# A four-layer network on one core: the convolution and the routing issued from written-out tables, experts' results laid out by partition, keys scaled on VectorE, and idle products ahead of the last keys

## The chip, the cores and the metric

The kernel runs on one core of one Trainium2 chip. The metric is device time in microseconds (us). In this text PE is the tensor engine, DVE is VectorE, ACT is ScalarE, POOL is GpSimd and SP is the engine that issues most of the DMA transfers. All data are float32.

## The reference

The input x has 8 sequences of 512 tokens with 128 features, 4096 tokens in all. Each of four layers works on a layer norm of x, and its result is added to x.

```python
x = x + conv(layernorm(x))        # sequence convolution with per-position weights
x = x + fp4_ffn(layernorm(x))     # gated FFN with FP4 rounding of inputs and weights
x = x + ttt(layernorm(x))         # attention by test-time training
x = x + experts(layernorm(x))     # 8 experts, 2 per token

# conv, per head of 8 features, K = 31 taps
avg    = cumsum(x) / (1, 2, 3, ...)
energy = stt + sigmoid(gate) * dyn            # dyn, gate = avg @ W_pe + b_pe
w      = softmax(energy over the 31 taps), zero where the tap lies before the start
out    = sum over taps of w[tap] * avg shifted by tap
v      = layernorm(out @ W_fc.T + residual) * gamma + beta

# ttt
q, k, v = x @ qkv_w + qkv_b ; q, k divided by their norm per head, scaled and shifted
for _ in range(2):                            # two steps of gradients and Newton-Schulz
    theta = theta - 0.1 * newton_schulz(grad of mean((silu(k@gate) * (k@val) @ proj - v)**2))
o = (silu(q @ gate) * (q @ val)) @ proj @ proj_w + proj_b

# experts
logits = x @ Wg + bg ; the two best of 8, gates by softmax over these two
pos    = place of (choice, token) in its expert, first all first choices, then all second
keep   = pos < capacity                       # 1229 rows for each expert
ye     = gelu(rows @ W1 + b1) @ W2 + b2       # for the rows of each expert
out[token] = sum over its two choices of gate * keep * ye[its row]
```

## The kernel before

The 4096 tokens lie in on-chip memory as `cx.x`, 128 partitions by NT = 32 tiles of 128 features; G = 4 tiles make a group of 512 tokens, and there are NG = 8 groups. Token number n * 128 + p stands in partition p of tile n. `Line` objects (`vec`, `ten`, `act`, `gp`) chain the instructions of one engine in the order in which the program issues them, so the order of those calls is the order on the engine. Where no Line is used, a scheduler orders the instructions by their dependences.

The profiled execution goes through these stages (us from the start of the span): convolution 0 to 234, FP4 FFN 234 to 376, keys 376 to 408, gradients and Newton-Schulz twice 407 to 926, output of the attention with the routing 930 to 1059, experts 1061 to 1222, last loads, adds and stores 1222 to 1240.

**Convolution** (`sequence_conv`). The features of one sequence are spread over partitions as (head, tap), four tap groups g = 0 to 3 (NGR = 4, of which NP = 3 weights are held in PSUM too). One pass of the loop L603-658 handles sequence b and, on the way, parts of others: `nxt` = b+1, `then` = b+2, `old` = b-1. For `cur`: `shared` lets POOL do a part of the products base * weights (L472), `product` does the others on VectorE (L483), `add_up` sums them over the taps on PE (cv, L492, eight matmuls a call), `part_sums` and `sums` make the softmax's denominators on PE with a copy dn on ACT (L439), `invert` takes the reciprocal rs on VectorE (L448), and `turn_inverse` turns it (rb) and copies it on ACT (rbs, L457). For `nxt` and `then`: `gates` and `taps` (matmuls and tanh), `energy` (en and the running maximum top, L395), `turn_top`, `greatest` (mx, L405) and `turn_greatest` (the maximum over taps, mb), `less` (subtract it) and `weigh` (exp on ACT). For `old`: `scale_down`, `project`, `norm1` (with statistics L263), and `finish` for b-2. `add_beta`, `scaled`, `means` belong to the neighbours b, b+4 and b+3. The sequence of these calls is written out in the loop by hand.

**Keys** (in `ttt`, L1236-1263). For each group: the k and v product; squares on ACT and their sums on VectorE (nrm); the copy of v to on-chip memory on VectorE (L1249); the scaling kt of the group before on ACT (L1196, `adjusted`); the root on ACT; the copy of a turned input; the division, which gives k (L1177, VectorE); four transposes of k on PE (tp, L1191). The first gradient's first product is `pa` (L1489).

**Output of the attention and routing** (L1290-1329, `Moe.route` L1650-1742). For each group the products pa and pb with the updated weights, silu on ACT (sw), the gated product ht on VectorE (L1317), the output product o on PE (L1322) and x = o + x (L1327). `moe.route(g - 1)` stands in front of the output product: transposes of x, statistics, a reciprocal root by `rsqrt` (L87-95), the logits (PSUM tile `both`, shared with the place sums), normalized rows xr on ACT, the choice of the two best (L1691-1697), counts (L1708-1712), place sums (L1716), slots (L1717-1727), and eight indirect DMA transfers from POOL's queue that write the rows to their slots in DRAM (L1732). A row carries the number of its token (`num`) and its gate. The transfers of second choices go first; each of those of first choices waits for the second choices of the group before (`after`).

**Experts** (`Moe.experts`, L1751-1865). For each expert its rows are loaded (`load`), in pieces of four tiles turned (`turn`: transposes and the copy xt, L1819), multiplied with W1 (ph, L1831), Gelu on ACT (ht), multiplied with W2 (po, L1844), biased and weighted on VectorE (ye, L1854 and L1856), and written by an indirect DMA of POOL's queue for each tile of 128 rows (L1858) to the row of its token: in `res` for the first six experts (one half for each choice), in an `own` buffer for each of the last two. The results are read back as y (L1805) and added to x (L1807): `behind` names the pieces after which this is done for res and the first own buffer, and a last loop does it for the last own buffer. Rows in res and own are in the order of the token numbers.

Of the kernel before, what the change touches and what calls it, by code (L numbers as in the profile page):

```python
# [1 line left out]

# [146 lines left out]
def sequence_conv(cx):  # L149
# [20 lines left out]
    BUSY = 14  # L170
    with ExitStack() as st:
# [430 lines left out]
        add_up(cur, 3)  # L602
        for b in range(1, B):  # L603
            cur, nxt, then, old = seq[b], seq.get(b + 1), seq.get(b + 2), seq.get(b - 1)
            shared(cur)
            product(cur, 0)
            if b > 1:
                finish(seq[b - 2], nc.gpsimd)
            part_sums(cur)
            sums(cur)  # L610
            if old:
                scale_down(old)
                project(old)
            add_up(cur, 0)
            if nxt:
                for g in (2, 3):
                    energy(nxt, g)
            invert(cur)
            if nxt:
                turn_top(nxt)  # L620
            if then:
                gates(then, 0)
            product(cur, 1)
            if nxt:
                greatest(nxt)
            turn_inverse(cur)
            if then:
                taps(then, 0)
            if nxt:
                turn_greatest(nxt)  # L630
            add_beta(b)
            add_up(cur, 1)
            if old:
                norm1(old, nc.gpsimd)
            if b + 4 < B:
                scaled(b + 4)
            if b == B - 3:
                ffn.load(flat(tri)[:, : ffn.NW], cur["spread"])
            if b >= B - 2:
                last_weights(cur)  # L640
                shared(cur, NP, NGR)
            product(cur, 2)
            add_up(cur, 2)
            if then:
                for g in (0, 1):
                    energy(then, g)
                gates(then, 1)
                taps(then, 1)
            if nxt:
                less(nxt)  # L650
                weigh(nxt, 0, 1)
            if b + 3 < B:
                seq[b + 3] = means(b + 3)
            if nxt:
                weigh(nxt, 1, NGR)
            if b < B - 1:
                product(cur, 3)
                add_up(cur, 3)
# [253 lines left out]
def fp4_ffn(cx):  # L912
# [7 lines left out]
        "H0 G2 H1 x0 G3 P0 T0 s0 S0 A2 A3 t0 H2 H3 D0 C0 P1 S1 d0 c0 T1 U0 D1 C1 T2 C2 g0 "  # L920
        "R0 R0 W0 K0 U1 f0 O0 u0 a0 f1 f2 W1 g1 K1 W2 K2 a1 W3 E0 K3 f3 K4 K5 K6 R1 K7 R1 "
        "r0 O1 r0 o0 "
# [210 lines left out]
def ttt(cx):  # L1133
# [10 lines left out]
    with ExitStack() as st:  # L1144
# [54 lines left out]
        with ExitStack() as s1:  # L1199
# [16 lines left out]
            FIRST, AHEAD = 4, 2  # L1216
# [23 lines left out]
            for g in range(NG):  # L1240
# [8 lines left out]
                vec(nc.vector.tensor_copy(grp(v, g), cur[:, :, D:]))  # L1249
                if g:  # L1250
                    act(adjusted(kt[:, (g - 1) * W : g * W], tk, 1))
# [4 lines left out]
                over_norm(cur[:, :, :D], root, nrm, grp(k, g), vec)  # L1256
                if g + AHEAD + 1 < NG:
                    normal(g + AHEAD + 1)
                tk = turn(ps, "t", grp(k, g), ten)
# [33 lines left out]
        with ExitStack() as s4:  # L1293
# [10 lines left out]
            for g in range(NG):  # L1304
                ht = p2.tile([P, NF, W], F32, tag="ht", name="ht")
                for c in range(NF):
                    pa = ps_h.tile([P, W], F32, tag="h", name="pa")
                    nc.tensor.matmul(
                        pa, gate[:, c * P : (c + 1) * P], qt[:, g * W : (g + 1) * W], start=True, stop=True
                    )  # L1310
                    pb = ps_h.tile([P, W], F32, tag="h", name="pb")
                    nc.tensor.matmul(
                        pb, val[:, c * P : (c + 1) * P], qt[:, g * W : (g + 1) * W], start=True, stop=True
                    )
                    sw = p2.tile([P, W], F32, tag="sw", name="sw")
                    nc.scalar.activation(sw, pa, AF.Silu)
                    nc.vector.tensor_tensor(ht[:, c, :], pb, sw, ALU.mult)  # L1317
                if g:
                    moe.route(g - 1)
                o = ps_o.tile([P, G, D], F32, tag="o", name="o")  # L1320
                for j in range(G):
                    for c in range(NF):  # L1322
                        nc.tensor.matmul(
                            o[:, j, :], ht[:, c, j * P : (j + 1) * P], w2[:, c, :],
                            start=(c == 0), stop=(c == NF - 1),
                        )
                nc.vector.tensor_tensor(grp(cx.x, g), o, grp(cx.x, g), ALU.add)  # L1327
            moe.route(NG - 1)
# [254 lines left out]

class Moe:
# [29 lines left out]
    def open_router(self, stack):  # L1614
# [27 lines left out]

        self.xr = cp.tile([P, K, NT, DX], F32, tag="xr", name="xr")
# [4 lines left out]
        self.seen = cp.tile([P, K, E], F32, tag="seen", name="seen")  # L1648
        nc.gpsimd.memset(self.seen, 0.0)
        self.limit = nc.gpsimd.to_reg(R - 1)  # L1650

    def route(self, g):
        cx = self.cx
        nc, tc, p2 = cx.nc, cx.tc, self.p2
# [266 lines left out]
```

## Time and profile before

| | |
|---|---|
| median of 3 runs | 1241.89 us (1241.77 to 1242.49) |
| profiled execution, its own time | 1242.03 us |
| its span on the core | 1240.3 us |
| mean granted PE clock | 0.965 |
| PE busy | 1097.9 us, 89% |
| VectorE busy | 754.0 us, 61% |
| POOL busy | 736.8 us, 59% |
| PE weight loads busy | 661.5 us, 53% |
| ACT busy | 488.0 us, 39% |

A share of busy time is a mean over all stages; the limit of a stage is seen only in a window of its own. A line of the timeline gives start and duration in us, the engine, the line of the kernel, the operation, output and inputs with their shapes, and in brackets the idle time before it and what ended it. A group of instructions gives the count, then the least, median and greatest duration in ns, and the first and last start. The clock is given as a share of full speed.

### The profile page before, as it was taken

The page shows a single profiled execution, that of the slowest core. Times are in us where ns is not written, and L with a number is a line of the kernel's source. Part 1 is how long each engine was busy: PE and PEld are TensorE (multiplying, and loading weights), DVE is VectorE, ACT ScalarE, POOL GpSimd, SP SyncE. Part 2 cuts the span into 40 slices and gives each one's busy share as a digit, 9 for nine tenths or more (in the row PEclk, how much of TensorE's full clock was granted, in tenths as well). Part 3 has the DMA queues.
Part 4 walks back from the last instruction along what each step waited for, and adds up shares of the span by engine and source line. Part 5 has one row for each costly group of instructions (what it writes and reads, how often), then busy time and mean ns, then how long its engine had stood idle before and what let it go on. Part 6 is the DMA issues. An engine that isn't in the chain of part 4 may idle for free.

```text
span 1240.3 us, 15590 instructions
## 1 busy us (share of the span) xinstructions
PE 1097.9 (89%) x5335; PEld 661.5 (53%) x5335; DVE 754.0 (61%) x1788; ACT 488.0 (39%) x1001; POOL 736.8 (59%) x720
## 2 busy tenths in 40 slices
PE   6999997858987899999988999999899993799992
PEld 4343432536666455555566455555576762577772
DVE  6899999988986544444455444444466785123354
ACT  4656554335657322232244232222343331243331
POOL 2266667635656888888822888888400656255553
PEclk9999999878999899999999999999999997799996
DMA  5324435860000000000000000000000111221277
GB/s 155 90 85 118 119 97 192 318 196 2 1 1 1 1 1 1 1 0 1 1 1 1 1 1 0 1 1 1 1 1 1 44 44 45 59 72 50 68 193 208
DMA packets 66894, 67.27 MB, mean 54 GB/s; under 512 B 6927, under 2 KB 48734, under 8 KB 66816
## 3 DMA queue, kind: packets, MB, share of 16 engines
q1 hardware_dynamic: 59296, 56.57, 15.3%
q0 software_dynamic: 4608, 8.43, 2.1%
q10 hardware_dynamic: 2912, 1.29, 0.4%
q8 instruction: 42, 0.69, 0.2%
q14 instruction: 36, 0.29, 0.1%
HBM read 40.00 MB, written 27.13 MB: 54 GB/s over the span
## 4 chain that ended last, share of the span: by engine, by line
PE 58%; DVE 21%; ACT 9%; issue 4%; POOL 3%; DMA 3%; ACTq 0%; DVEq 0%; POOLq 0%; SPq 0%
PE ph L1537 5%; PE sum L1512 5%; PE po L1844 4%; PE pp L1527 4%; PE sum L1511 4%; PE sum L1513 4%; PE ph L1831 4%; PE pa L1489 4%; PE pb L1491 4%; DVE v L858 3%; PE cv L492 2%; DVE pr L483 2%; PE pt L1520 2%; PE gu L974 1%; DVE ht L1317 1%
## 5 line engine op out<-in xcount | busy, mean ns | idle before, releaser
L1502 POOL TENSOR_TENSOR ds<-sw,s 128x512 f32<-128x512 f32 x64 | 81.7, 1276 | 86.3 <-DVE sw L1497 86.3
L1504 POOL TENSOR_TENSOR ds<-ds,s 128x512 f32<-128x512 f32 x64 | 111.6, 1744 | 5.0
L1732 POOL DMA_INDIRECT rows<-xr,slot x64 | 62.9, 983 | 73.8 <-DVE rs L95 45.1
L1495 ACT COPY b<-pb 128x512 f32<-128x512 f32 x64 | 37.5, 586 | 162.1 <-PE pb L1491 161.5
L1858 POOL DMA_INDIRECT res<-ye,xe x60 | 58.4, 974 | 66.2 <-DVE ye L1856 28.1
L472 POOL TENSOR_TENSOR pr<-base,en 128x512 f32<-128x512 f32 x52 | 74.9, 1474 | 36.9 <-ACT en L428 36.5
L1499 DVE TENSOR_TENSOR h<-sw,b 128x512 f32<-128x512 f32 x64 | 50.2, 785 | 70.6 <-ACT b L1495 70.1
L1834 ACT ACTIVATE ht<-ph,b 128x512 f32<-128x512 f32 (+2 forms) x100 | 56.1, 588 | 93.5 <-PE ph L1831 92.0
L483 DVE TENSOR_TENSOR pr<-base,w 128x3072 f32<-128x3072 f32 (+2 forms) x27 | 86.3, 3206 | 0.8 <-ACT w L426 0.8
L1503 POOL TENSOR_TENSOR ds<-sw,ds 128x512 f32<-128x512 f32 x64 | 82.8, 1294 | 5.0
L1505 POOL TENSOR_TENSOR ds<-ds,b 128x512 f32<-128x512 f32 x64 | 81.6, 1274 | 5.0
L1527 PEld LDWEIGHTS pp<-proj,ht 128*128 128x128 f32 x512 | 67.1, 191 | 30.7 <-issue 29.8
L1844 PE MATMUL po<-w,ht 128*128 128x128 f32 (+1 forms) x640 | 77.8, 278 | 0.0
L1522 ACT COPY ht<-pt 128x512 f32<-128x512 f32 x64 | 37.6, 587 | 101.5 <-PE pt L1520 101.5
L1497 DVE TENSOR_TENSOR sw<-pa,s 128x512 f32<-128x512 f32 x64 | 44.2, 691 | 53.7 <-ACT s L1493 53.7
L1831 PE MATMUL ph<-xt,w 128*128 128x512 f32 (+2 forms) x200 | 73.4, 511 | 3.4 <-DVE xt L1819 3.4
L1844 PEld LDWEIGHTS po<-w,ht 128*128 128x128 f32 (+1 forms) x640 | 74.6, 189 | 0.7
L1539 DVE TENSOR_TENSOR db<-ph,sw 128x512 f32<-128x512 f32 x64 | 44.2, 691 | 47.2 <-PE ph L1537 47.2
L1537 PE MATMUL ph<-proj_t,dpt 128*128 128x512 f32 x128 | 71.6, 641 | 0.0
L492 PE MATMUL cv<-pr,sel 128*32 128x512 f32 x512 | 62.4, 616 | 8.6 <-DVE pr L483 8.6
L1489 PE MATMUL pa<-gate,kt 128*128 128x512 f32 x128 | 66.8, 604 | 2.5 <-ACT b L1495 2.4
L1512 PE MATMUL sum<-db,k 128*128 128x512 f32 x128 | 66.2, 598 | 1.6 <-DVE db L1539 1.6
(359 smaller groups left out, 2545.6 us busy)
## 6 DMA issues: line engine op xcount, KB each, us to landing
base<-far SPq DMA_DIRECT2D x64, 268.0 KB, 5.2
rows<-empty SPq DMA_DIRECT2D x1, 5005.0 KB
res<-zero SPq DMA_DIRECT2D x1, 4096.0 KB, 26.3
own<-zero SPq DMA_DIRECT2D x2, 2048.0 KB, 18.8
w<-in_L_ffn_W SPq DMA_DIRECT2D x16, 256.0 KB, 4.8
y<-res SPq DMA_DIRECT2D x16, 256.0 KB, 5.5
xe<-rows SPq DMA_DIRECT2D x7, 585.0 KB, 4.3
y<-own SPq DMA_DIRECT2D x12, 256.0 KB, 4.7
```

Source lines behind the costliest of these rows:

```text
L483: vec(nc.vector.tensor_tensor(s["pr"][g][:, lo:hi, :], s["base"][:, lo:hi, at], w.to_broadcast([P, hi - lo, L]), ALU.mult))
L492: ten(nc.tensor.matmul(s["cv"][32 * j : 32 * (j + 1), :], sel[:, i].rearrange("p a h -> p (a h)"), s["pr"][g][:, i * NJ + j, :], start=(g ...
L1489: nc.tensor.matmul(pa, ki, gate, start=True, stop=True)
L1502: nc.gpsimd.tensor_tensor(ds, sw, s, ALU.mult)
L1503: nc.gpsimd.tensor_tensor(ds, sw, ds, ALU.subtract)
L1504: nc.gpsimd.tensor_tensor(ds, ds, s, ALU.add)
L1505: nc.gpsimd.tensor_tensor(ds, ds, b, ALU.mult)
L1512: nc.tensor.matmul(sums[1], ki, db, **kw)
L1527: nc.tensor.matmul(pp, ht[:, c * P : (c + 1) * P], proj[:, c, :], start=(c == 0), stop=(c == NF - 1))
L1537: nc.tensor.matmul(ph, dpt, proj_t, start=True, stop=True)
L1831: ten(nc.tensor.matmul(ph[:, :n], self.w1[:, e, c * P : (c + 1) * P], xt[:, :n], start=True, stop=True))
L1844: ten(nc.tensor.matmul(po[:m, i - lo, :], ht[:, c, (i - lo) * P : (i - lo) * P + m], self.w2[:, e, c, :], start=(c == 0), stop=(c == NF - ...
```

## The change

It has five parts.

1. The convolution's loop is issued from a table `ORDER`; a letter names the call, a digit its tap group. Against the old sequence, rs comes one energy earlier and mx behind the statistics of pj on VectorE; add_up of group 1 comes ahead of rb, ev and mb on PE; dn is copied ahead of four operations of `finish`, and the rows xn of `scaled` ahead of rbs, on ACT; the exps are taken in the order of groups 1, 3, 2.
2. Keys: kt of groups 0 to 6 is scaled by VectorE, the copy of v stands behind k, and twelve products of the identity with itself go ahead of the last group's transposes.
3. Output and routing are issued from two tables with Lines on three engines; `Moe.route` becomes a class `Route`. The last group is worked on in two halves. Three copies go from VectorE to ACT (the second set of rows, the second choice and the two gates), the logits have a PSUM tile of their own, and the wait of the first choices' transfers is taken by one memset on POOL ahead of them. A Gelu of one column is issued on ACT at the end of the stage.
4. Tokens are numbered p * 32 + n, so that the 4 tiles of a group in one partition are one stretch of 2 KB in res and own.
5. The last expert's first piece of four tiles becomes two pieces of two, and `behind` is adapted.

```diff
+    ORDER = (
+        "S0 P0 D0 n0 N0 F0 J0 e2 A0 v0 e3 t0 g0 g1 P1 A1 Z0 L0 X0 T0 P2 s0 i0 k0 k1 m0 B0 A2 E0 E1 g2 g3 "
+        "k2 k3 l0 w0 M0 w1 w3 w2 p3 a3 "
+    )
...
         for b in range(1, B):
             cur, nxt, then, old = seq[b], seq.get(b + 1), seq.get(b + 2), seq.get(b - 1)
-            shared(cur)
-            product(cur, 0)
-            if b > 1:
-                finish(seq[b - 2], nc.gpsimd)
-            part_sums(cur)
-            sums(cur)
...
+            parts = dict(
+                S=(cur, lambda s, g: shared(s)), p=(cur if b < B - 1 else None, product), P=(cur, product),
+                a=(cur if b < B - 1 else None, add_up), A=(cur, add_up), n=(cur, lambda s, i: part_sums(s)),
+                N=(cur, lambda s, i: sums(s)), v=(cur, lambda s, i: invert(s)), i=(cur, lambda s, i: turn_inverse(s)),
+                X=(cur if b >= B - 2 else None, lambda s, i: more_shared()),
+                D=(old, lambda s, i: scale_down(s)), J=(old, lambda s, i: project(s)),
+                Z=(old, lambda s, i: norm1(s, nc.gpsimd)), F=(seq.get(b - 2), lambda s, i: finish(s, nc.gpsimd)),
+                e=(nxt, energy), t=(nxt, lambda s, i: turn_top(s)), T=(nxt, lambda s, i: greatest(s)),
+                m=(nxt, lambda s, i: turn_greatest(s)), l=(nxt, lambda s, i: less(s)),
+                w=(nxt, lambda s, g: weigh(s, g, g + 1)),
+                g=(then, gate), k=(then, tap), E=(then, energy),
+                M=(b + 3 if b + 3 < B else None, lambda b, i: mean(b)), s=(b + 4 if b + 4 < B else None, lambda b, i: scaled(b)),
+                B=(b, lambda b, i: add_beta(b)), L=(b if b == B - 3 else None, lambda b, i: load_ffn()),
+            )
+            for name in ORDER.split():
+                at, part = parts[name[0]]
+                if at is not None:
+                    part(at, int(name[1]))
...
-            FIRST, AHEAD = 4, 2
+            FIRST, AHEAD, BUSY = 4, 2, 12
...
-                vec(nc.vector.tensor_copy(grp(v, g), cur[:, :, D:]))
                 if g:
-                    act(adjusted(kt[:, (g - 1) * W : g * W], tk, 1))
+                    vec(nc.vector.tensor_scalar(
+                        kt[:, (g - 1) * W : g * W], tk, cols[:, 1, 0:1], cols[:, 1, 1:2], ALU.mult, ALU.add
+                    ))
...
                 over_norm(cur[:, :, :D], root, nrm, grp(k, g), vec)
+                vec(nc.vector.tensor_copy(grp(v, g), cur[:, :, D:]))
                 if g + AHEAD + 1 < NG:
                     normal(g + AHEAD + 1)
+                if g == NG - 1:
+                    busy = ps.tile([P, W], F32, tag="t", name="busy")
+                    for _ in range(BUSY):
+                        ten(nc.tensor.matmul(busy[:, :P], cx.ident, cx.ident, start=True, stop=True))
                 tk = turn(ps, "t", grp(k, g), ten)
...
+            ORDER = (
+                "a2 t0 a4 H1 u0 a2 S1 l0 b1 G0 b8 H2 S2 b4 G1 b1 H3 n0 S3 n1 n2 n3 m0 c7 G2 c1 d4 G3 O0 "
+                "O1 d3 e6 v0 O2 O3 f6 x0 f2 h0 s0 "
+            )
+            LAST = (
+                "a1 H1 S1 t0 u0 a6 G0 H2 S2 a1 l0 b9 b4 G1 b1 H3 c1 S3 n0 n1 G2 c1 n2 n3 m0 G3 c2 O0 O1 "
+                "c4 d1 x0 T0 U0 d1 A1 d1 A1 d1 A2 d3 L0 e1 B1 e1 B1 e1 B1 e3 v0 B5 f1 B2 f1 B1 f1 B1 f1 "
+                "B1 f1 B1 N0 N1 C1 f1 C1 f2 C1 M0 C5 D7 E4 V0 F8 "
+            )
+            vec, ten, act = Line(tc), Line(tc), Line(tc)
+            parts = [(g * G, G) for g in range(NG - 1)] + [(NT - G, G // 2), (NT - G // 2, G // 2)]
...
+                parts = dict(zip(T, (lambda s, i, f=f: getattr(s["route"], f)() for f in ("turn", "turned", "logits", "spread", "sums"))))
+                parts[T[5]] = lambda s, j: s["route"].normal(j)
+                parts.update((c, step(name)) for c, name in zip(t, ("stats", "roots", "first", "second", "before", "places")))
...
+                table = dict(
+                    H=(s, hidden), S=(s, silu), G=(s, gated), O=(s, out_of), x=(s, lambda s, i: add(s)),
+                    h=(nxt, hidden), s=(nxt, silu), **routing(old, "abcdef", "tulmvn"),
+                    **(routing(s, "ABCDEF", "TULMVN") if nxt is None else {}),
+                )
...
+            ahead = wp.tile([P, 1], F32, tag="ahead", name="ahead")
+            act(nc.scalar.activation(ahead, cx.eps[1e-5], AF.Gelu_apprx_tanh))
...
+class Route:
...
+    def spread(self):
+        self.act(self.moe.cx.nc.scalar.copy(self.rows[1][:, :, :D], self.rows[0][:, :, :D]))
...
+        pl = m.ps_t.tile([P, W], F32, tag="t", name="pl")[:, : self.n * E]
...
+        self.act(nc.scalar.copy(self.hot[:, K], self.hot[:, K - 1]))
...
+            self.act(nc.scalar.activation(self.rows[k][:, :, D + 1], dif, AF.Copy, bias=0.5, scale=s))
...
+        for k in (1, 0):
+            if k == 0 and lo:
+                gate = nc.gpsimd.memset(self.small("gate", 1), 0.0)
+                m.after(gate, m.scatters[-1][: len(m.scatters[-1]) // K])
...
-        nc.gpsimd.iota(num, [[T, K], [P, NT]], base=0, channel_multiplier=1)
+        nc.gpsimd.iota(num, [[T, K], [1, NT]], base=0, channel_multiplier=NT)
...
-        res = self.slots.res.rearrange("(k n p) d -> p k n d", k=K, p=P)
-        sums = [res[:, k] for k in range(K)] + [t.rearrange("(n p) d -> p n d", p=P) for t in self.slots.own]
+        res = self.slots.res.rearrange("(k p n) d -> p k n d", k=K, p=P)
+        sums = [res[:, k] for k in range(K)] + [t.rearrange("(p n) d -> p n d", p=P) for t in self.slots.own]
...
-            for lo, hi in (((0, G), (G, 2 * G), (2 * G, NR)) if e < E - 1 else ((0, G), (G, G + 2), (G + 2, G + 4), (G + 4, NR)))
+            for lo, hi in (((0, G), (G, 2 * G), (2 * G, NR)) if e < E - 1 else ((0, 2), (2, G), (G, G + 2), (G + 2, G + 4), (G + 4, NR)))
...
-        behind = {first + i: (i // 2, i % 2) for i in range(2 * (K + OWN - 1))}
+        behind = {first + at: (i // 2, i % 2) for i, at in enumerate((0, 1, 2, 3, 5, 6))}
```

In the tables of part 3 the letters H, S, G, O and x are the hidden products, silu, gated products, output products and the add of the part at hand, h and s the first hidden product and silu of the next one, and t, u, l, m, v, n and a to f the routing of the part before: transposes, their copy, logits, spread copy, place sums, normalized rows, and (with a number of VectorE steps) statistics, roots, first choice, second choice, counts and places. The capital T, U, L, M, V, N and A to F do the same for the very last half. The route's operations are those of `Moe.route` apart from what part 3 names.

## The prediction

> **What bounds the kernel now.** I read the page first: its 40 slices (31.0 us each) show which engine a stage leans on.
>
> ```profile
> PE   6999997858987899999988999999899993799992
> DVE  6899999988986544444455444444466785123354
> PEclk9999999878999899999999999999999997799996
> DMA  5324435860000000000000000000000111221277
> ```
>
> The convolution (slices 1 to 7) has PE and VectorE (DVE) both at 9; the two gradient stages are PE's and untouched; the routing slices (31 to 34) end in PE 3, DVE 5, clock 7: a tail in which neither works. The last two slices belong to DMA. So five stretches are touched, each with its own bound, and I asked for the windows of each (us; then PE, PEld, DVE, ACT, POOL busy; clock; DMA share; GB/s):
>
> ```profile
> 123.39:149.72 26.33, 24.58 (x132) 10.49 (x132) 25.48 (x25) 15.20 (x28) 16.02 (x27) 1.00 0.37 97
> 404.20:407.50 3.30, 0.63 (x4) 0.43 (x5) 2.60 (x5) 0.90 (x2) 3.22 (x3) 0.74 0.00 0
> 407.50:410.40 2.90, 2.88 (x7) 1.87 (x8) 0.00 (x0) 0.79 (x2) 1.76 (x3) 0.50 0.00 0
> 955.00:1032.50 77.50, 75.00 (x382) 50.30 (x380) 61.14 (x349) 28.12 (x60) 45.31 (x47) 1.00 0.12 40
> 1032.50:1058.70 26.20, 4.02 (x20) 2.95 (x20) 10.30 (x68) 2.44 (x6) 17.58 (x18) 0.59 0.15 48
> 1207.00:1222.50 15.50, 10.35 (x73) 9.39 (x71) 11.23 (x23) 4.54 (x12) 11.79 (x10) 0.97 0.57 162
> 1222.50:1240.30 17.80, 0.00 (x0) 0.00 (x0) 5.45 (x8) 0.00 (x0) 0.00 (x0) 0.50 0.85 238
> ```
>
> One convolution step is 26.33 with VectorE busy 25.48. Around the first gradient PE waits, then runs at half clock. Six routing groups cost 77.5, PE 75.0 of it. The last experts lean on POOL's issues, the end on DMA.
>
> **Convolution (L603-658).** ORDER moves, on VectorE, two operations; nothing is added.
>
> ```profile
> 124.49 0.56 DVE L448 RECIPROCAL rs<-sm 128x64 f32<-128x64 f32 x1 [0.16 <-PE sm L444]
> 128.81 0.69 DVE L405 TENSOR_REDUCE mx<-tt 128x64 f32<-128x512 f32 x1 [0.55 <-PE tt L400]
> L395 DVE SCALAR_TENSOR_TENSOR top<-en,bias,top x24: 750/863/1803, 19.4 to 201.8; 128x512 f32<-128x512 f32 x24
> ```
>
> Since VectorE is short by only 0.85 a step, its waits are the step's cost. mx goes behind four statistics of pj (0.88, already there), which covers its wait of 0.55 in four steps; rs goes one energy earlier, and weigh's exps two late, so the 0.16 in three steps goes: 4 x 0.55 + 3 x 0.16 = 2.7. On ACT (15.20 of 26.33 busy) the copies and exps only change places, and PE's eight add_up products go ahead of three short ones; cover is ACT's 11 of idle time. If that cover were gone, the wait would show as pr on w, which is 0.8 in 27 products now. POOL's beta add (1.28) moves behind the last steps' products; its cover is the same slack (16.02 of 26.33). One size is not shown: L395 takes 750 alone and up to 1803 beside POOL's products, and its partner changes with the order. Bounds for all 24: -5 (the median's 0.11 and the long ones gone) to +2 (eight more at the 0.23 of the 978 ones); I take 0, as the number of POOL products is unchanged. Conv: -2.7.
>
> **Keys (L1236-1263).** kt of seven groups goes from ACT to VectorE, and the copy of v (0.68) behind the k product.
>
> ```profile
> L1196 ACT ACTIVATE kt<-tp,cols x8: 763/777/778, 384.1 to 408.6; 128x512 f32<-128x512 f32 x8
> 407.52 1.09 PE L1191 MATMUL tp<-ident,k 128*128 128x128 f32 x4 [2.65 <-DVE k L1177]
> ```
>
> kt's 0.777 on ACT mostly lies beside VectorE's sum of squares, so ACT's loop loses little: in the last two groups the root waited for kt, 0.35 and 0.2; sum -0.6. VectorE's added kt (estimate 0.68, as the v copy of the same shape) takes the place of the copy. Twelve idle products then go into the 2.65 before the last transposes: by the four transposes in 0.63 of the group before, 12 x 0.16 = 1.9, which fits and leaves 0.8 idle. With the clock kept, these transposes take 0.63 as in the group before instead of 1.09, and the first product of the gradient, now 1.06, about 0.6 (its mean in the page's L1489 row): 0.46 + 0.46 and a second product's start, 1.1. Against this stands the Trainium skill, "TensorE: Matmul & The Clock Gate", Part 1: the clock falls only after an idle window of about 3.4 us, so a gap of 2.65 alone shouldn't lower it, and the products would bring nothing (-0.6 in all). The rows above show clock 0.74 and 0.50 right behind that gap; I go by them: keys -1.7.
>
> **Routing (L1290-1329, L1650-1742).** Before, PE sets the period, 12.76 to 13.2 a group, and VectorE waits once:
>
> ```profile
> 976.73 0.19 DVE L1680 TENSOR_TENSOR lg<-both,rs 128x32 f32<-128x32 f32 x1 [1.92 <-PE both L1678]
> 976.96 0.19 DVE L1681 TENSOR_TENSOR lg<-lg,L_ffn_bg 128x32 f32<-128x32 f32 x1
> L90 DVE TENSOR_SCALAR rs<-rs x8: 159/170/454, 946.0 to 1035.7; 128x4 int32<-128x4 int32 x8
> L1732 POOL DMA_INDIRECT rows<-xr,slot x64: 969/972/1232, 960.7 to 1056.3; - x64
> ```
>
> The first two rows give the price of a dependent operation: 0.225 from start to start though it is busy 0.19. The new ORDER takes three copies (xr, hot, weights) to ACT (28 of 77.5 busy, so covered) but issues long runs of dependent ones on VectorE: statistics 1.2, 14 root steps x 0.207 = 2.9, 14 choosing steps x 0.22 = 3.0, counts 1.2, places 1.05, four gated products net 0.5 = 2.0, the add 0.68, plus waits for the place sums (0.5) and the last output products (0.5): 13.0, and 0.2 for shared access with POOL: 13.2 a group, as before. PE needs 12.2. So six groups gain nothing; x of group 6 lands at 941.8 + 6 x 13.2 = 1021.0 (before 1019.3, +1.7).
>
> The gain is the tail. Now group 7's route starts at 1032.5 and its eight scatters come behind group 6's:
>
> ```profile
> 1046.06 2.30 DMA rows<-xr,slot
> 1056.28 2.28 DMA rows<-xr,slot
> 1058.70 2.58 DMA xe<-rows
> ```
>
> The last group becomes two halves. The first half's x comes 13.2 less the halved gated products (1.2) and outputs (0.7) later: 1032.3. The second half adds statistics, roots, choices and gated halves of 6.8: 1039.1. Its own route to the first slot, 14 x 0.2 + 14 x 0.2 + 4 x 0.2 + places, sums and waits 4.6: 11.0, so 1050.1; then four issues at 1.28 (0.97 + 0.31) start until 1053.9, and landing takes 2.3: 1056.2 instead of 1058.6. Routing: -2.4. Bounds: -5 (PE's 12.4 sets the period) to +3 (0.75 a group more). The eight added memsets ("gate") each hold POOL until the former group's scatters have landed, which the first k=0 scatter did itself; behind them stand only scatters of the same queue, so I cost them at 0; without that cover 0.3 each, of which the last two count. The Gelu table's early load (now 1.3, beside half-clock products at 1065) is hidden both ways: 0.
>
> **Experts and end (L1751-1865).**
>
> ```profile
> PE ph L1831 <- DVE xt L1819: 2.6, 2, 2.0
> q1 hardware_dynamic: 6336, 3.15, 68.8%
> q1 hardware_dynamic: 3193, 6.47, 105.0%
> ```
>
> PE's 2.0 wait is for an xt copy behind four adds that wait for y loads. With 2 KB rows loads come faster, so I halve it: -1.0; the other 0.5 goes with the shifted adds. The last expert's ten scatters run without a gap on POOL from 1207.9 to 1222.4, and the last ye is ready at 1219.0; with the first piece halved they start some 3 earlier, so the last two issues follow ye and start 1.1 earlier. The y loads and adds of the last two groups keep their places (offsets 5 and 6 for a piece more); only offset 3's four adds (2.5 on VectorE) now stand ahead of the second half piece's ye instead of behind it, while POOL issues the first half's two scatters (2.8): 0, and 2.5 on two scatters if that cover were gone, of which the 3 in hand would take all. SP's queue holds nothing else there. Experts -2.6.
>
> The y loads: the last two rows (packets, MB, share of 16 engines) are 1224 to 1240 in packets of 512 bytes, and 222 to 238 in 2 KB: 0.688 x 256 us / 6336 = 27.8 ns against 1.05 x 256 / 3193 = 84 ns. Eight last loads: 4096 x 27.8 / 16 = 7.1 against 1024 x 84 / 16 = 5.4: -1.7, of which I take 1.5, as adds and stores follow. Against it: "DMA: Bandwidth & Descriptors", Specifications, has full rate from 512 bytes on, by which regrouping is worth 0; the rows differ (295 against 390 GB/s over 16 engines, from the same numbers), though one is a write of zeros. Rows of one scatter now lie 16 KB apart instead of side by side; no row shows that. It is between 0 and +0.9 for the last landing (the 3.2 maximum of L1732's landings against 2.3); I take 0.
>
> **Sum.** -2.7 - 1.7 - 2.4 - 2.6 - 1.5 = -10.9 from the profiled 1242.03: 1231.1. The median of the runs is 0.14 lower: 1231.0.
>
> **Rivals.** A, slower: a POOL issue of an indirect DMA holds VectorE. L90's one 454 against 170 is such a meeting, 0.28; long runs of dependent operations leave it no slack, so eight issues a group cost 2.2, less the 0.2 counted, times seven: +14.5, 1245.5. It decides from a period of 13.2 + 13.4 / 7 = 15.1 on. For it: VectorE has no idle 1.9 left. Against: the same eight issues lie beside the same operations now, and most aren't lengthened. Chance 0.14.
> B: the tops lengthen to their bound (+2) and the routing chain takes 0.4 more a group (+2.8): conv and routing give nothing, 1235.8. Chance 0.15.
> C: the tops shorten by 3 and PE sets the routing period (-5 instead of -2.4): 1225.4, with the lower bound of the tops 1223. Chance 0.10.
> D: the change doesn't do what it says: the idle products don't hold the clock (+1.1) and y loads run no faster (+2.5): 1234.6. Chance 0.06.
> The forecast itself, 1227 to 1235: 0.55.
>
> **Numbers.** 0.2%, about what a measurement of this kernel can tell from no change, is 2.5: 1239.4 and 1244.4. Slower: A's upper part, 0.14. Same: A's rest and B's worst, 0.06. Faster: 0.80. The range 1221 to 1242 leaves out C's lower part (0.04) and most of A (0.13).
>
> **What would show it.** mx without a wait; clock above 0.9 from 404 to 410; adds of x 13.2 apart and the last scatter starting near 1054 on the old clock, so some 1049.5 after the earlier gains; ph waiting 1 instead of 2; y in 2 KB packets. A spacing above 15, lengthened small operations beside L1732, or tops over 0.98 make it wrong.

## The result and the profile after

The changed kernel took 1251.70 us (median of 6 runs, 1247.61 to 1253.07) against 1241.89 for the kernel before: ratio 1.0071, interval 1.006 to 1.0083. The forecast was 1231.0, in a range from 1221 to 1242. The change is slower. The profiled execution took 1253.07, with a span of 1251.4 and a mean clock of 0.956 (before: 0.965).

The page of the changed kernel, busy tenths in 40 slices (31.3 us each):

```profile
PE   7999998767987899999988999999989996699992
DVE  6899889977997744444445544444455888133364
PEclk8999898877999999999999999999999998799997
```

PE's row looks almost as before. The row to read is PEclk: it was 9 in the first seven slices, and now shows 8 in slices 1, 5 and 7 (slice 8 was 8 before, too). The convolution runs with PE's clock lowered again and again; the routing and the last experts look as before or better.

I cut both profiled executions at the same events (starts of the first rs, the last pj product, the first pa of the gradients, the last ph, the first output product, the first transpose of the experts' rows, the last result scatter, the end):

| stretch | before | after | difference | forecast |
|---|---|---|---|---|
| start to the first rs (no instruction changed) | 46.8 | 49.4 | +2.6 | 0 |
| convolution loop, first rs to last pj | 192.0 | 206.3 | +14.3 | -2.7 |
| FFN and keys, to the first pa | 169.6 | 168.9 | -0.7 | -0.6 |
| gradients, to the last ph | 481.3 | 480.5 | -0.8 | -1.1 |
| Newton-Schulz, to the first output product | 48.1 | 48.1 | 0 | 0 |
| output and routing, to the experts' first transpose | 123.6 | 121.3 | -2.3 | -2.4 |
| experts, to the last scatter's issue | 160.1 | 158.9 | -1.2 | -2.6 |
| end | 18.8 | 18.0 | -0.8 | -1.5 |

The sum is +11.1, the difference of the spans. The stretches behind the convolution all have the forecast sign, though the experts' -1.2 lies within the spread of that stretch, as is shown below; the convolution alone decides. The first 2.6 are not the change's: the instructions there are the same, the clock happened to be 0.66 from 15 to 20 us, and over the seventeen profiles of this study the first rs starts anywhere between 46.5 and 51.1.

One step of the convolution, from rs to rs, window of the changed kernel (us; PE, PEld, DVE, ACT, POOL busy; clock; DMA share; GB/s); then two VectorE lines of the timeline in that kernel, and VectorE's waits from 40 to 235:

```profile
128.94:157.91 28.97, 27.05 (x132) 12.08 (x132) 25.11 (x24) 15.05 (x28) 15.73 (x27) 0.90 0.32 89
```

```profile
111.96 0.75 DVE L394 SCALAR_TENSOR_TENSOR en<-ev,bias,sg 128x512 f32<-128x512 f32 x1 [1.01 <-PE ev L362]
128.94 0.56 DVE L453 RECIPROCAL rs<-sm 128x64 f32<-128x64 f32 x1 [2.08 <-PE sm L449]
```

```profile
DVE rs L453 <- PE sm L449: 6.1, 5, 2.1
DVE en L394 <- PE ev L362: 3.8, 4, 1.1
DVE en L394 <- ACT sg L370: 2.6, 1, 2.6
DVE mx L410 <- PE tt L405: 0.9, 1, 0.9
```

VectorE's work is the same as before (25.11 against 25.48), but the step is 2.6 longer. mx, which the change was to free, waits once only. The wait has moved to rs: in the old order it came behind the second energy and waited 0.16 there, now it comes 1.7 earlier (en and top) and waits up to 2.08, for sums that are not ready any sooner. PE's busy time rose from 24.58 to 27.05 with the same 132 records (a product has two): that is the clock, 0.90.

Where the clock falls is seen around sm. Windows of the changed kernel (first two rows) and of the kernel before (last two), cut at the pn products and five us on:

```profile
153.90:157.90 4.00, 2.39 (x13) 1.11 (x12) 2.27 (x3) 2.82 (x7) 4.00 (x4) 1.00 0.97 291
157.90:162.90 5.00, 4.68 (x28) 3.52 (x32) 4.95 (x4) 0.88 (x2) 4.73 (x4) 0.66 0.65 201
```

```profile
146.90:150.90 4.00, 2.89 (x15) 1.45 (x15) 3.78 (x5) 2.77 (x7) 4.00 (x4) 1.00 0.99 291
150.90:155.90 5.00, 5.00 (x39) 2.96 (x39) 4.45 (x4) 0.62 (x1) 4.66 (x4) 1.00 0.73 190
```

PE does the four pn products and sm as ACT delivers the exps. In the new order two pn products stand behind the last exp (group 2's, where it was group 3's), with holes of 0.9 and 0.7 in PE: 60% busy in these 4 us against 72% before. Right behind, the clock is 0.66 in the one kernel and 1.00 in the other.

### The profile page after: what moved, and what is told of

Read it like the earlier page. It is cut to its first block, busy times and chain, and to the rows that moved or that the text cites. A ratio compares the mean times of both kernels' runs of the same rounds, so it can differ in the third digit from the quotient of the medians.

```text
span 1251.4 us, 15736 instructions
## 1 busy us (share of the span) xinstructions
PE 1113.2 (89%) x5387; PEld 679.8 (54%) x5387; DVE 768.6 (61%) x1808; ACT 493.9 (39%) x1041; POOL 739.5 (59%) x728
## 4 chain that ended last, share of the span: by engine, by line
PE 52%; DVE 16%; ACT 4%; POOL 3%; issue 3%; DMA 2%; DVEq 0%; ACTq 0%; POOLq 0%; SPq 0%
PE ph L1583 5%; PE sum L1558 5%; PE pp L1573 4%; PE sum L1557 4%; PE sum L1559 4%; PE po L1962 4%; PE pa L1535 4%; PE ph L1949 4%; PE pb L1537 4%; DVE v L842 3%; PE pt L1566 2%; PE o L1331 2%; DVE ht L1324 1%; PE gu L957 1%; PE a L1423 1%
## 5 line engine op out<-in xcount | busy, mean ns | idle before, releaser
L1548 POOL TENSOR_TENSOR ds<-sw,s 128x512 f32<-128x512 f32 x64 | 81.4, 1272 | 86.1 <-DVE sw L1543 86.1
L1551 POOL TENSOR_TENSOR ds<-ds,b 128x512 f32<-128x512 f32 x64 | 81.4, 1272 | 5.0
L497 PE MATMUL cv<-pr,sel 128*32 128x512 f32 x512 | 66.2, 639 | 9.5 <-DVE pr L488 9.3
```

The costliest lines, as they stand in the source:

```text
L1548: nc.gpsimd.tensor_tensor(ds, sw, s, ALU.mult)
L1551: nc.gpsimd.tensor_tensor(ds, ds, b, ALU.mult)
```

## The experiments

The runs below were made on four chips (on record as 3, 7, 9 and 13), on each of which the kernel before takes 1272 to 1276, not 1242 as in the result above. A ratio is to the kernel before on the same chip, with a 95% interval of about 0.002 to either side. The convolution does not differ (its loop takes 192.0 in the first profile of the kernel before, 192.1 in the one on chip 13, and 192.3 and 192.1 with the old table on chips 3 and 7), so I compare the loop, from the start of the first rs to that of the last pj product. The difference of 30 us lies in the routing; it is taken up at the end.

A loop is that of one execution. The changed kernel's own took 206.3 in the first profile and 203.3 in the second (after2), and the second profile is of the fastest of its seven executions (1260.58, median 1265.19). So a difference of 3 between loops says little alone, and the ratios are read beside it.

| version | loop | clock in steps 1 to 6 | total, ratio to before |
|---|---|---|---|
| old table (c_old) | 192.3 | 1.0 in all | 1252.11, 0.9825 |
| new table (after2) | 203.3 | 1.0, 1.0, .94, .92, .90, .87 | 1265.19, 0.9934 |
| exps back (w_back) | 200.1 | 1.0, 1.0, .94, 1.0, .94, .94 | 1259.12, 0.9888 |
| reciprocal back (rs_back) | 203.0 | 1.0, 1.0, .93, .89, .94, .86 | 1263.62, 0.9913 |
| add_up back (cv_back) | 202.7 | 1.0, 1.0, 1.0, .94, 1.0, 1.0 | 1263.46, 0.9925 |
| exps and reciprocal back (wr) | 199.9 | 1.0, 1.0, .94, 1.0, 1.0, .88 | 1257.56, 0.9859 |
| all three back (wrc) | 200.6 | 1.0, 1.0, .94, 1.0, 1.0, 1.0 | 1261.67, 0.9897 |
| old table, mx and dn moved (mx_dn) | 198.0 | 1.0, 1.0, 1.0, 1.0, .94, .94 | 1254.44, 0.9851 |
| new table, much filler (fill) | 206.4 | 1.0 in five, .94 | 1264.08, 0.9923 |
| new table, little filler (fill1) | 197.2 | 1.0 in five, .94 | 1256.19, 0.9846 |
| old table, little filler (c_old_fill) | 195.8 | 1.0 in all | 1252.74, 0.9838 |
| exps back, little filler (w_fill) | 197.3 | 1.0 in five, .94 | 1256.51, 0.9878 |
| exps and reciprocal back, little filler (wr_fill) | 198.2 | 1.0 in five, .94 | 1259.22, 0.9895 |

**Is it the table?** Everything of the change but the convolution's order (the line with a minus is the changed kernel's):

```diff
-"S0 P0 D0 n0 N0 F0 J0 e2 A0 v0 e3 t0 g0 g1 P1 A1 Z0 L0 X0 T0 P2 s0 i0 k0 k1 m0 B0 A2 ... w1 w3 w2 p3 a3"
+"S0 P0 F0 n0 N0 D0 J0 A0 e2 e3 v0 t0 g0 g1 P1 T0 i0 k0 k1 m0 B0 A1 Z0 s0 L0 X0 P2 A2 ... w1 w2 w3 p3 a3"
```

> The changed kernel with the convolution's table in the old order (ORDER = the sequence of calls of before); the other four parts of the change stay. Both theories: the whole loss is the convolution's (its end 238.8 before, 255.7 after), the rest gained 5.7, so about 1236. If instead the other parts only look faster because they follow a slow convolution, 1240 or more.

The total, 1252.11, would by its number be the second branch, but both were for the first chip, and here the kernel before takes 1274; the loop is back at 192.3 with all clocks at 1.0. Ratio 0.9825 (0.9806 to 0.9844). The changed kernel itself, on such a chip (13):

> The changed kernel once more, on one chip with the others. Where the kernel before takes 1242 it should take 1251 (ratio 1.007). Where the kernel before takes 1274, as beside the last four runs, whose routing groups came 14.4 apart instead of 13.05: the version with the old convolution took 1252 there, and the new table costs 15 in the convolution, so 1267, which would be a gain of 0.5%.

It took 1265.19, ratio 0.9934 (0.9916 to 0.9952): there the change is a gain, and the table costs 13.1 of it (11.0 by the loops). One step of each, the old table first:

```profile
125.78:152.11 26.33, 24.58 (x133) 10.49 (x133) 25.49 (x24) 15.19 (x28) 16.02 (x27) 1.00 0.34 93
125.94:154.43 28.49, 26.30 (x133) 12.42 (x134) 25.38 (x24) 15.57 (x29) 16.67 (x27) 0.92 0.33 91
```

**One move at a time.** Three explanations stand against each other: W, rs waits for late sums; C, holes in PE lower its clock; P, PE's new order delays what VectorE waits for. First the exps (`w1 w3 w2` to `w1 w2 w3`):

> The changed kernel with only the order of the exps put back (w1 w2 w3 instead of w1 w3 w2), so that one denominator product instead of two is left behind the last exp. Theory W (the wait alone): sm comes 0.6 earlier in five steps, 3 less: about 1249. Theory C (PE's holes ahead of sm let the clock fall, and half clock makes the holes of the next step): the hole gets shorter, the clock stays at 1.0 in most steps, about 1241. Rival P (PE's order, add_up ahead of rb and ev): no change, 1251.

Then the reciprocal (`v0 e3` to `e3 v0`):

> The changed kernel with only the reciprocal put back behind the second energy (e3 v0 instead of v0 e3). Theory W: the waits of rs for sm (0.6 to 2.1 in four steps, 6 in all) are halved or go, about 1246. Theory C: PE's holes ahead of sm stay, as they are set by ACT's exps, so the clock still falls: 1248 to 1251. Rival P: 1251.

Then PE's order (`P1 A1 Z0` to `P1 Z0`, and `B0 A2` to `B0 A1 A2`):

> The changed kernel with only add_up of group 1 put back on PE behind rb, ev and mb. Rival P: ev is 1.9 earlier, the waits of en for ev (0.8 to 1.1 in four steps) go, and with them what follows on ACT and PE: about 1241 with the clock near 1.0. Theory W: only 4 less, 1247. Theory C without P: 1250, clock as low as before in steps 3 to 6.

No move carries the loss. The exps give 3.2 in the loop and 6.1 in the total (0.9888, 0.9869 to 0.9907), between the 3 of theory W and the 10 of theory C, and the clock still falls in three of six steps. The reciprocal and add_up give 0.3 and 0.6 in the loop, and their ratios (0.9889 to 0.9936, 0.99 to 0.995) cannot be told from the changed kernel's. With the reciprocal put back, rs waits 1.0 in all instead of 9.7, but mx waits 6.6 for tt and en 4.6 for ev: the wait goes to the next instruction that needs PE, whose clock is as low as before. So theory W, which asked for over 5 here, fails, and P as the single cause with the run of add_up.

That run is a miss of theory C too, which expected the clock as low as before. It is at 1.0 in five of six steps, as P expected, and still the loop is no shorter; this step of it is at full clock:

```profile
100.22:128.47 28.25, 24.21 (x132) 10.44 (x132) 26.07 (x25) 15.30 (x29) 15.89 (x29) 1.00 0.34 96
```

Here en's wait is gone, but rs waits 8.9 (2.7 with the old table), and the 24 tops on VectorE take 26.4 in all instead of 22.9. By estimate from these figures the two make 9.6 of the 10.4 by which this loop is longer than the old table's. A full clock is therefore not enough: an order can lose as much by late sums and by VectorE's work becoming longer beside POOL's.

Two windows of w_back show about what a fall of the clock costs, as they hold the same 132 records:

```profile
99.40:127.55 28.15, 26.55 (x132) 12.00 (x132) 25.27 (x24) 15.30 (x29) 17.50 (x30) 0.94 0.29 83
127.55:154.07 26.52, 24.80 (x132) 10.47 (x132) 25.06 (x24) 15.30 (x29) 16.50 (x27) 1.00 0.36 100
```

The step without a fall is 1.6 shorter.

**Moves together.**

> The changed kernel with two of the table's moves put back: the exps in the order 1 2 3, and the reciprocal behind the second energy. The loop (from the first rs to the last pj product) is 192 with the old table and 203 to 206 with the new one; each move alone put back gave 200.2 and 203.0. If the late denominators are the cause (theory W), both together give 195 or less and the clock stays at 1.0; if PE's order (add_up ahead of rb, ev and mb) is the cause (theory P), mx then waits for tt and en for ev as with the reciprocal alone put back: 199 to 203.

> The same with the third move put back too, add_up of group 1 behind rb, ev and mb; mx behind the statistics, dn ahead of finish's operations and xn ahead of rbs stay. If these three moves carry the loss, the loop takes 192 to 194 as with the old table. If the moves that stay carry a part (the run with mx, add_up ahead of mb alone and dn moved took 198), it takes 196 to 199, with tops of 1.8 and the clock falling in some steps.

The loops take 199.9 and 200.6, both over what theory W asked for, with a fall of the clock in the third step (and in wr in the sixth). wr lies where P expected it, but wrc, which gives PE its old order too, is no shorter and misses both of its branches. By its total wr has won back 7.6 of the 13.1 (0.9859, 0.9842 to 0.9875). In wrc a new wait appears, pr for w (4.1 in two steps): with PE's old order and the moves that stay, the exps are late for VectorE's product, and the tops take 25.7. Of the moves that stay, those of xn, of scale_down (D0) and of the first add_up (A0) were never tried alone.

**The part that looked safest.** The old table with mx behind the statistics of pj, add_up of group 1 ahead of mb alone and dn ahead of finish's operations:

```diff
-"S0 P0 F0 n0 N0 D0 J0 ... P1 T0 i0 k0 k1 m0 B0 A1 Z0 s0 L0 X0 P2 ..."
+"S0 P0 n0 N0 F0 D0 J0 ... P1 i0 k0 k1 B0 Z0 T0 A1 m0 s0 L0 X0 P2 ..."
```

> The changed kernel with a third table: the old one with three moves alone, mx behind the statistics of pj, add_up of group 1 ahead of mb alone, and dn ahead of finish's four operations. The waits of mx (0.55 in four steps) and rs (0.15 in three) should go: convolution 2.7 shorter than with the old table, end at 237.7 or less, total 2.7 under the run with the old table on the same chip. Rival: the later mx makes mb, less and the exps late and the time comes back at rs: no gain or a loss.

The first of these two windows of it is a step at full clock, the second the next one:

```profile
124.63:150.87 26.24, 24.82 (x132) 10.47 (x132) 25.93 (x25) 15.31 (x29) 15.86 (x27) 1.00 0.35 95
150.87:178.70 27.83, 26.44 (x132) 11.26 (x132) 25.92 (x24) 13.75 (x25) 15.67 (x27) 0.94 0.30 84
```

In the first the waits of mx and rs are gone, 0.71 together, and the step is 0.1 shorter than with the old table (26.34): VectorE's busy time rose by 0.45 instead. The timeline shows where: the top beside POOL's products takes 1792 to 1799 ns in three steps, and 1450 to 1460 with the old table, and cs waits 0.16. This is the bound of the prediction's rival B, and here it ate the gain. Then the clock falls, and the loop takes 198.0, where 2.7 less than with the old table was expected.

**Filling PE's holes.** If the clock is the cause, work that nobody needs must make the kernel faster. In `part_sums` the second product is repeated, in `sums` products of the identity go into sm's tile before its own:

```diff
-            for g in range(NGR):
+            for g in (0, 1, 1, 1, 2, 3):
...
             s["sm"] = sm = ps_m.tile([P, G, H], F32, tag="m", name="sm")
+            for _ in range(6):
+                ten(nc.tensor.matmul(flat(sm), cx.ident, cx.ident[:, : G * H], start=True, stop=True))
```

> The changed kernel with filler on PE: two repeats of pn's second product ahead of its third, and six 128x64 products of the identity ahead of sm, where PE waits for ACT now. The results of the filler are overwritten. Theory C (the clock): PE's holes of 0.9 and 0.7 are filled, the clock stays at 1.0 through the steps, and with it 7 to 9 of the 15 lost in the convolution come back: its end at 247, the waits of rs stay. Theory W (the wait alone): no gain, or 0.3 a step of loss by the filler: end at 256 to 258.

The time came out as theory W said, no gain (206.4), and the clock as C said, 1.0 in five of six steps. rs waits 18.5 in all. The likely reason, found after the result, is that this much filler is itself in sm's way. Less of it, `(0, 1, 1, 2, 3)` and two products:

> The changed kernel with less filler on PE than before: one repeat of pn's second product and two 128x64 products ahead of sm (0.4 and 0.3). Theory C: the clock stays near 1.0 and the filler, which is shorter than the holes, costs nothing: the loop takes 198 to 200 instead of 203. Theory W: no gain, 203 to 206, rs waits as in the changed kernel (9 to 10 in all).

The loop takes 197.2 instead of 203.3, the ratio is 0.9846 (0.9825 to 0.9868) instead of 0.9934. The step that answers to the 28.49 of the changed kernel, and rs's wait over the loop:

```profile
127.20:153.70 26.50, 25.44 (x139) 10.96 (x139) 24.51 (x25) 15.31 (x28) 17.73 (x28) 1.00 0.33 94
DVE rs L455 <- PE sm L451: 10.7, 7, 3.8
```

Three products more (six records) and 2 us less. rs waits as long as without filler (9.7), so its wait is not what was won; the waits of en and mx for PE, 4.5 together in after2, are gone. The control, the same filler where the clock is at 1.0 without it:

> The version with the old convolution table, with the filler that shortened the loop of the new table from 203 to 197 (one repeat of pn's second product, two 128x64 products ahead of sm). The old table's clock is 1.0 already. Theory C (filler helps by the clock alone): nothing to gain here, loop 192 to 196, as the 0.4 and 0.3 lie in holes or push sm back by that. Rival R (the filler helps by itself, for instance by spacing PE's work): loop under 190.

```profile
126.03:152.83 26.80, 25.33 (x139) 11.17 (x139) 25.49 (x25) 15.22 (x28) 16.05 (x27) 1.00 0.32 94
```

The loop takes 195.8, 3.5 more than without: the filler by itself costs time, so what it brings the new table it brings by the clock. 6.1 of the 11.0 is shown so, and the ratios' intervals of the new table with and without filler do not meet. With filler the two tables are 1.4 apart, so by estimate some 9.6 of the 11.0 is the clock (6.1 gained although 3.5 was paid; that these add is worked out, not shown).

What is left of the difference:

> The new table with the exps in the order 1 2 3 and the filler. With the clock held, what is left is the wait of rs for sm: the order 1 2 3 leaves one product behind the last exp instead of two, 0.5 a step in five steps: loop 194 to 195, against 197.2 with the filler alone, clock 1.0. If the clock falls again, 198 to 200.

> The new table with the exps in the order 1 2 3, the reciprocal behind the second energy, and the filler. If the early reciprocal is the rest of the loss once the clock is held, the loop is 190 to 193, as good as the old table or better; if PE's order (add_up ahead of rb and ev) costs by itself, en waits 0.8 to 1.1 for ev in four steps and it is 195 to 197.

Both missed: 197.3 and 198.2 (the second is nearest to its branch for PE's order: en waits 3.2 for ev in four steps). With the clock held, steps 3 and 4 take 26.5 with the new table wherever exps and reciprocal stand (26.54, 26.55 and 26.52 in the fourth), and 26.8 with the old one and filler. What is left lies in steps 6 and 7, of which the sixth still has a fall. No gain from rs's place is seen.

**The results' layout.** The old table with rows of res and own in token order:

```diff
-        nc.gpsimd.iota(num, [[T, K], [1, NT]], base=0, channel_multiplier=NT)
+        nc.gpsimd.iota(num, [[T, K], [P, NT]], base=0, channel_multiplier=1)
```

and "(k n p) d", "(n p) d" for "(k p n) d", "(p n) d".

> The version with the old convolution table, with the results' rows laid out in token order as before (512-byte rows in the y loads). The prediction gave the new layout 1.5 at the end and 1.0 in the experts: 2.5 slower than the version with the new layout (1252.1). The traces of the changed kernel gave 0.8 and 1.2 for all that was done to experts and end, so by them 1 to 2. If rows of 512 bytes run at the full rate anyway: no difference.

It took 1253.34, ratio 0.982 (0.9799 to 0.9841), not distinguishable from 0.9825, and not the 2.5 slower that the prediction's gains asked for. In the traces the stretch from the last scatter's issue to the last add is 12.1 here, 11.8 and 11.7 in the kernel before, and 10.9 to 11.3 in every version with the new layout: a gain of 0.8 to 1.2, under what the totals can tell.

**The other chips.**

> The kernel before once more, for its trace beside the others. If the kernel before takes 1274 here again, theory S (a product's signal reaches VectorE late while PE goes on without a pause, in the routing alone) expects routing groups of some 17 instead of 13.1, all other stages as in the first profile; theory T (the whole chip is slower) expects every stage to be 2.6% longer.

Theory S holds: of the 30.0 by which the span is longer than in the first profile, 29.5 lie between the first output product and the experts' first transpose. Most routing groups are 18.7 to 19.2 apart, more than the 17 expected. Three lines of this execution, of PE, VectorE and POOL; "remote" stands where the trace names no instruction that ended a wait:

```profile
998.14 2.70 PE L1323 MATMUL o<-w,ht 128*128 128x128 f32 x22
1005.73 0.69 DVE L1327 TENSOR_TENSOR x<-o,x 128x512 f32<-128x512 f32 x1 [4.27 <-remote]
1003.34 0.97 POOL L1732 DMA_INDIRECT rows<-xr,slot  x1 [0.30 <-issue]
```

The products are done at 1000.8 and VectorE begins to add at 1005.7; in the records PE's signals come in a bunch at that moment. The POOL line is the last of a group's eight scatters. All five such waits of VectorE end 2.4 to 2.5 after the start of that last scatter, about when it lands (a landing took 2.3 in the first profile). So the signals come when the run of scatters is over; no run tests whether it holds them.

The changed kernel's groups are 14.3 apart there, and 13.05 on the first chip. So the new routing, with its halved last group, gains 2.3 on one chip and some 20 on the other. The prediction did not have this gain. Why the signals come late on these chips stays open, and with it whether the gain is the kernel's or theirs.

## Why the prediction was wrong

**The convolution.** Two steps of the sum failed. The first: "rs goes one energy earlier ... so the 0.16 in three steps goes" took a small wait for a sign that sm is ready by then. It is ready when ACT's last exp and the products behind it are done. dn ahead of finish's operations brings that forward, the new order of the exps pushes it back; in the two timelines dn ends 0.5 earlier in the step, and rs stands 1.7 earlier. The rest is the new wait (8.6 in the loop of the first profile, 2.7 before). So at full clock the new order is worth little: with the same filler, steps 3 to 5 take 26.5, 26.5 and 26.1 against 26.8 with the old one, 1.2 in three steps where the sum had counted 0.7 in each.

The second and larger: VectorE was taken for the only bound, and PE's and ACT's moves were given a price of nothing, "cover is ACT's 11 of idle time". PE was busy 24.58 of 26.33, and its idle time was no free cover. The clock record of the traces goes by stretches of 3.4 us. In steps 2 to 5 of the changed kernel half clock follows stretches with PE busy 0.62, 0.54, 0.70 and 0.64 of the time, in which no single hole is longer than 0.9. In the kernel before, the emptiest stretches of steps 1 to 6 are 0.61, 0.62 and 0.67 busy, and there the clock stays, so the busy share alone does not decide. Over the loops of all seventeen profiles, full clock was lost behind all 35 stretches under 0.45, behind 31 of the 116 from 0.45 to 0.70, and behind 1 of the 785 above that. What decides in between stays open. A fall makes PE late for tt and ev (with filler those waits are gone); that it also makes the next hole was expected, but in w_back a step at full clock follows one with a fall. The price of holes was missing from the sum altogether, though the prediction had costed exactly this effect 300 us later, in the keys. In the prediction's terms -2.7 became +14.3 in the first profile and +11.0 in the second; of the 11.0, 6.1 is shown to be the clock and some 9.6 estimated.

Neither rival A nor B named it. B's tops have a share in the first profile, where their sum is 24.5 us (22.9 before), near its bound of +2; in the second profile of the changed kernel it is 22.7, and the loss is there all the same.

The Trainium skill, "TensorE: Matmul & The Clock Gate", Part 1, lowers the clock after an idle window of about 3.4 us; by that rule alone the loop would have kept its clock and the term stood at what the waits cost. The same part also reports a kernel whose clock swung with frequent short idles, without a size for them. Here the clock fell behind stretches that were over half busy, so the measurement decides: in this loop holes of 0.3 to 0.9 were enough.

**Keys.** Here the prediction went by the row against the rule, and the second profile of the kernel before shows what that row was worth. Its two windows at that place, without any idle products:

```profile
405.53:408.83 3.30, 0.63 (x4) 0.42 (x4) 2.73 (x6) 1.12 (x3) 3.19 (x3) 1.00 0.00 0
408.83:411.73 2.90, 2.35 (x8) 1.07 (x8) 0.28 (x1) 1.69 (x2) 2.24 (x3) 1.00 0.00 0
```

The gap is the same, and the clock does not fall (first gradient up to its ninth pa: 24.9, against 25.8 in the first profile, and 25.0 with the idle products in all versions). So the idle products gained 0.8 of the forecast 1.1 against the first execution and nothing against the second: that this term came out was luck in part. The emptiest stretch of 3.4 us was 46% busy where the clock fell and 45% where it stayed; what decides stays open.

**Routing.** Right, by its own steps. Adds of x came 13.05 apart (forecast 13.2), the two halves 11.3 and 6.9 behind (11.3 and 6.8), the last four scatters' first 11.0 behind that (11.0):

```profile
1047.14 0.42 DVE L1339 TENSOR_TENSOR x<-o,x 128x256 f32<-128x256 f32 x1
1054.06 0.42 DVE L1339 TENSOR_TENSOR x<-o,x 128x256 f32<-128x256 f32 x1
1065.04 0.97 POOL L1780 DMA_INDIRECT rows<-xr,slot  x1 [0.27 <-issue]
```

The stretch gained 2.3 against 2.4. Rival A, POOL's issues holding VectorE, did not come (its own terms give 14.0, not 14.5). This holds for the first profile alone; on the other chips the groups are 14.3 apart.

**Experts.** Half wrong. PE's wait for xt was to be halved; it rose:

```profile
PE ph L1949 <- DVE xt L1937: 4.5, 4, 1.7
```

from 2.6 in two waits. The two half pieces put more xt copies behind adds on VectorE, and offset 3's four adds, which the prediction gave no cost, stand there; that is read from the order of the instructions and was not tried. The last scatters still came earlier, and -1.2 was left in this profile; but over all profiles with the new experts the stretch spreads from 158.0 to 162.4 (160.1 in both of the kernel before), so no gain of this part is shown.

**End.** The right way, half the size: the last y load landed in 6.3 instead of 7.3, and the stretch gained 0.8 instead of 1.5. Packets of 2 KB were priced from a transfer that only writes.

**A better version.** The old table with the other parts, c_old, beats both kernels where it was run: 0.9825 against 0.9934 for the change and 1 for the kernel before. On the first chip it was not run; the traces there give 1242.0 less 5.8, about 1236, as an estimate.

## What to carry to other kernels

Before an instruction is moved ahead, ask when its input is produced, not how long it waits now: if the producer doesn't move, a wait only changes its place. In a loop where PE is nearly full, small holes in PE are not free: look at the granted clock behind each of them, and keep PE's busy share over some 3.4 us up (above 70% the clock of these loops held in all but one of 785 stretches), with filler if need be. Keep the filler small: 0.7 us a step helped here, and more than twice as much gave no gain. An order that is good on paper for one engine must be costed on all engines that share the loop; with add_up put back the clock was up and the loop as slow.

## What the hardware showed unexpectedly

- The clock fell behind stretches of 3.4 us in which PE was 54 to 70% busy, by records whose ends are modelled. Of all such stretches from 45 to 70%, three in four kept it, and above 70% all but one of 785 did.
- Filler of some 0.7 us a step took 6.1 us off the loop where the clock fell (9 us off the total), and the same filler cost 3.5 in the loop where the clock was up already.
- The kernel before takes 1242 on one chip and 1272 to 1276 on others, nearly all of the difference in one stage, where VectorE waits up to 4.3 us for PE's signals, until a run of eight scatters has ended; the changed kernel loses 13 there. So the same change is 0.7% slower on one chip and 0.7% faster on another.
